# Mixing expert weights on TensorE in column quarters, with the first load in four parts

## The chip, the cores and the metric

The kernel runs on one core of a Trainium2 chip. A core has four engines that compute (TensorE, short PE, multiplies matrices; VectorE, DVE; ScalarE, ACT; GpSimd, POOL) and a fifth, SyncE (SP), that here only issues DMA transfers. Each engine works through its own instructions in order and waits on semaphores for the others. The metric is the device time of one execution in microseconds, the median over several runs.

## The reference

Four layers are applied to x, of 4 images with 512 channels of 64 x 64 points, all in float32. Only layer 1 has to be seen in detail:

```python
# layer 0: attention inside each image, 64 channels wide: softmax over 4096 x 4096 scores
x = scale * (w_out @ (value @ softmax(key.T @ query))) + x
# layer 1: a convolution block whose weights are mixed per image from E = 8 experts
rw = sigmoid(mean(x) @ router_w.T + router_b)         # [image, expert]
W  = einsum('be,eoihw->boihw', rw, experts)           # for each of w1, w2, w3
x  = relu(bn(conv1x1(relu(bn(conv3x3(relu(bn(conv1x1(x, W1))), W2))), W3)) + x)
# layer 2: linear attention;  layer 3: projection, two discounted running sums, a gate
```

w1 has 128 x 512 weights per expert, w2 128 x 128 x 9 and w3 512 x 128. The mixing of experts is a sum over e of rw[b, e] times the weights of expert e; it can only start when the mean over the image of layer 0's output is known.

## The kernel before

The function `unshifted` does the work. `tile_kernel` calls it, and then a second, slower form only if a range test fails, which it doesn't here. TensorE's instructions stand in the order in which the program text issues them (`manual_schedule` around the loop over images, line 859). VectorE's stand in program order inside the blocks marked so; elsewhere, and for ScalarE in layers 0 to 2, a scheduler orders them.

An image is held as four x tiles of 128 x (4 x 1024), one per pair of 512-point blocks ("pr" 0 to 3). Images after the first are loaded during layer 3 of the image before. For the first, `load_pair` (line 81) issues one 2 MB transfer per tile, after the 384 KB of wqkv_sb; the projection in `project_in` (line 170) takes 128 channels (kc) of a tile at a time.

Experts are stored as 17 pieces ("j") of 128 input rows x 8 experts x 128 output columns: 4 for w1, 9 for w2, 4 for w3. Their mixing takes two forms:

- Pieces 0 to 3 are loaded early in layer 0 (ex0, line 159). At the end of layer 0, lines 329 to 337 make rw from the pooled sums, lines 338 to 340 make eight diagonal matrices rw[e] * identity on VectorE, and TensorE sums diag[e] times the expert's pieces over e in PSUM (line 345). ScalarE copies the result to wc (line 360).
- Pieces 4 to 16 go through `mix_experts` (line 361): a load, one scaled copy on ScalarE (line 365), and seven multiply-adds on VectorE (line 367). It runs for pieces 4 to 6, 7 to 9 and 10 to 12 in layer 1, and for 13 to 16 (w3) as `mix_last`, placed after `sums_of_six(2)` (line 566).

conv1 (line 395) multiplies the x tiles with pieces 0 to 3, all four pairs one after another; ScalarE writes h1. conv2 is a 3 x 3 convolution by a fast algorithm along the rows: `sums_of_six` (line 408, VectorE) makes six combinations of h1, lines 382 to 388 make combinations of the nine pieces of w2 (taps), TensorE multiplies (line 448), VectorE combines back (lines 451 to 458), ScalarE makes h (line 462). conv3 multiplies with pieces 13 to 16 (line 471), and VectorE adds x (line 473).

Buffers matter to the loads. `bigp` has three buffers, which in layer 0 hold the keys, queries with values, and part of a ring of exponentials; `xpool` has five, four x tiles and another part of the ring. A load of experts waits until one of these is free. In PSUM, `pair_psum` has three buffers of two banks and `bank` two of one bank. At the start of a run, VectorE and ScalarE also make the batch-norm constants (lines 127 to 134), and ScalarE sums the last two x tiles (line 284).

An f32 product appears in the trace as two TensorE instructions, each with its weight load. Where the output takes 64 of the 128 columns, two products on the two halves stand side by side.

Of the kernel before, what the change touches and what calls it, by code (L numbers as in the profile page):

```python
# [8 lines left out]
F32 = mybir.dt.float32  # L9
AF = mybir.ActivationFunctionType  # L10
ALU = mybir.AluOpType
AX = mybir.AxisListType
# [3 lines left out]
P = 128  # L16
HW = H * W
NB = 512
NBLK = HW // NB
ROWS = NB // W  # L20
KC = C // P
# [3 lines left out]
NPAIR = NBLK // 2  # L25
E = 8
NPIECE = KC + 9 + KC
# [16 lines left out]

@with_exitstack
def unshifted(ctx: ExitStack, tc: tile.TileContext, fits, x, wqkv_t, wout_t, router_t,
                experts, wqk_t, wv_t, bv, wproj_t, prm, out):


    nc = tc.nc  # L50
# [24 lines left out]
    def late_weights(src, shape, name):  # L75

        t = wlate.tile(shape, F32, tag="late", name=name)
        nc.sync.dma_start(t, src)
        return t

    def load_pair(b, pr):

        t = xpool.tile([P, KC, 2 * NB], F32, tag="x", name=f"x_{b}_{pr}")
        nc.sync.dma_start(t, x[b, :, pr * 2 * NB:(pr + 1) * 2 * NB].rearrange("(kc p) n -> p kc n", p=P))
        return t


# [54 lines left out]
    def router_of_values():  # L142
# [9 lines left out]
                             start=kc == 0, stop=kc == KC - 1)  # L152
        nc.vector.tensor_scalar(wr_sb, wo_t[:, 1, 0:E], col(SCALE), 1.0 / HW, ALU.mult, ALU.mult)

    def layer0(b, xs):


        tc.keep_in_program_order(nc.scalar.preload_act_table_set("natural_log_exp_and_others"))
        ex0 = late_weights(experts[0:KC].rearrange("n p e c -> p n e c"), [P, KC, E, P], f"ex_{b}_0")
# [158 lines left out]


        pr = NPAIR - 1  # L320
        for i in groups[-1]:
            values(i)
        with tc.manual_schedule(engines={mybir.EngineType.DVE}):
            sums(pr, early=False)
            for m in range(KC):
                y = out_product(pr - 1, m)
                nc.scalar.activation(ring[8 + m], y, AF.Copy, scale=col(SCALE))
            ys = [out_product(pr, m) for m in range(2)]
            prod = small.tile([P, E], F32, tag="prod", name=f"prod_{b}")
            nc.vector.scalar_tensor_tensor(prod, wr_sb, osum[:, 1:2], base, ALU.mult, ALU.add)  # L330
            logit = bank(f"logit_{b}", (P, E))
            nc.tensor.matmul(logit, ones, prod, start=True, stop=True)
            rw = small.tile([P, E], F32, tag="rw", name=f"rw_{b}")
            nc.vector.tensor_tensor(rw, logit, col(RB, E), ALU.add)
            nc.scalar.activation(rw, rw, AF.Exp, scale=-1.0)
            nc.vector.tensor_scalar(rw, rw, 1.0, None, ALU.add)
            nc.vector.reciprocal(rw, rw)
            diag = four(f"diag_{b}").rearrange("p h (e c) -> p (h e) c", c=P)
            for e in range(E):
                nc.vector.tensor_scalar(diag[:, e, :], ident, rw[:, e:e + 1], None, ALU.mult)  # L340
            ys.append(out_product(pr, 2))
            add_out(pr, 0, ys[0])
            mix = bank(f"mix_{b}", (P, KC, P))
            for e in range(E):
                nc.tensor.matmul(mix, diag[:, e, :], ex0[:, :, e, :], start=e == 0, stop=e == E - 1)
# [7 lines left out]
        return rw, mix  # L353

    def layer1(b, xs, rw, mix):

        wcq = bigp.tile([P, NPIECE + 1 + 4 * NPAIR, P], F32, tag="big", name=f"wc_{b}")
        wc = wcq[:, 0:NPIECE, :]
        qs = wcq[:, NPIECE + 1:, :].rearrange("p (a j) c -> p a (j c)", a=NPAIR)
        nc.scalar.copy(wc[:, 0:KC, :], mix)  # L360
        def mix_experts(j, n, pool, tag):
            ex = pool.tile([P, 4, E, P], F32, tag=tag, name=f"ex_{b}_{j}")
            nc.sync.dma_start(ex[:, 0:n], experts[j:j + n].rearrange("n p e c -> p n e c"))
            acc = wc[:, j:j + n, :]
            nc.scalar.activation(acc, ex[:, 0:n, 0, :], AF.Copy, scale=rw[:, 0:1])
            for e in range(1, E):
                nc.vector.scalar_tensor_tensor(acc, ex[:, 0:n, e, :], rw[:, e:e + 1], acc,  # L367
                                               ALU.mult, ALU.add)
# [12 lines left out]
        part = block(f"part_{b}", (P, 4, P))[:, 0:3, :]  # L381
        nc.scalar.activation(taps[:, 0], g0, AF.Copy, scale=0.25)
        for k, c0, c1 in ((1, -1 / 6, 1 / 6), (3, 1 / 24, -1 / 12)):
            c2 = -1 / 6 if k == 1 else 1 / 6
            nc.scalar.activation(part, g0, AF.Copy, scale=c0)
            nc.vector.scalar_tensor_tensor(part, g2, c2, part, ALU.mult, ALU.add)
            nc.vector.scalar_tensor_tensor(taps[:, k], g1, -c1, part, ALU.mult, ALU.add)
            nc.vector.scalar_tensor_tensor(taps[:, k + 1], g1, c1, part, ALU.mult, ALU.add)


        h1 = bigp.tile([P, 4, H, W // 4 + 1], F32, tag="big", name=f"h1_{b}")
# [81 lines left out]
                nc.vector.scalar_tensor_tensor(xm, flat(y), bn_s[:, 2 + m:3 + m], xm, ALU.mult, ALU.add)  # L473
                nc.scalar.activation(xm, xm, AF.Relu, bias=bn_t[:, 2 + m:3 + m])

        return conv1, sums_of_six, lambda: mix_experts(13, 4, bigp, "big"), conv2, conv3, wcq, qs

    def layer2(b, xs, conv1, sums_of_six, mix_last, conv2, conv3, wcq, qs):

        ks = small.tile([P, NPAIR], F32, tag="ks", name=f"ks_{b}")  # L480
        g = bank(f"g_{b}", (P, C))
# [75 lines left out]
        def ahead(pr):  # L557
            return [lambda j=j: move(pr, j) for j in range(2)]

        for pr in range(NPAIR):  # L560
            conv1(pr)
        with tc.manual_schedule(engines={mybir.EngineType.DVE}):
            sums_of_six(0)
            sums_of_six(1)
            sums_of_six(2)
            mix_last()
            h2 = {0: conv2(0)}
            sums_of_six(3)
            h2[1] = conv2(1)
            conv3(0, h2[0])  # L570
# [305 lines left out]

@with_exitstack
def general(ctx: ExitStack, tc: tile.TileContext, x, wqkv_t, wout_t, router_t,
                experts, wqk_t, wv_t, bv, wproj_t, prm, out):

    nc = tc.nc
    const = ctx.enter_context(tc.tile_pool(name="g_const", bufs=1))
# [432 lines left out]
```

## Time and profile before

| | |
|---|---|
| median of 3 runs | 2747.29 us (2745.97 to 2748.14) |
| profiled execution | 2749.85 us |
| its span, first to last instruction | 2748.1 us |
| mean granted TensorE clock | 0.997 |
| instructions in the trace | 25459 |
| mixing on VectorE, line 367, per image | 21 of 128 x 384 at 0.62 us, 7 of 128 x 512 at 0.76 us |
| mixing on TensorE, line 345, per image | 16 instructions, from 310.82 to 317.88 us in the first image |
| first TensorE instruction | 9.16 us |

A row of the page's costliest groups shows how it is written:

```profile
L471 PE MATMUL c<-h,wc 128*128 128x512 f32 x256 | 118.7, 605 | 11.2 <-DVE x L473 5.8
```

Line 471 on TensorE writes the tile c from h and wc, with weights of 128 rows x 128 columns and 512 data columns, 256 times: 118.7 us busy, 605 ns of one; before these, the engine sat idle for 11.2 us, of which VectorE's writing of x at line 473 ended 5.8. The 605 ns overlap with the next instruction, since matmuls are pipelined; the distance between starts is the true pace.

### The profile page before, as it was taken

What the parts mean: (1) busy time and instruction counts of PE and PEld (TensorE: products, weight loads), DVE (VectorE), ACT (ScalarE), POOL (GpSimd) and SP (SyncE); (2) the same over time, 40 slices, a digit from 0 to 9 for tenths busy, and PEclk for the clock granted to TensorE, in tenths of its full rate; (3) what the DMA queues carried; (4) which work ended last, traced back from release to release, by engine and by line L of the source; (5) the groups of instructions that cost most, each with busy time, mean ns of one, the idle gap of its engine ahead of it and who ended that gap; (6) DMA issues with size and microseconds to landing.
All of it is one profiled execution on the core that took longest, in us unless ns stands there. A gap on an engine that the chain in (4) does not pass through costs nothing.

```text
span 2748.1 us, 25459 instructions
## 1 busy us (share of the span) xinstructions
PE 2682.6 (98%) x9918; PEld 1119.6 (41%) x9918; DVE 1991.3 (72%) x2259; ACT 1310.9 (48%) x1491; POOL 10.7 (0%) x26
## 2 busy tenths in 40 slices
PE   8999999999999999999999999999999999999998
PEld 3333354344333345434433334544443333554443
DVE  2688776787478777678747778767874787866787
ACT  4545344445554434345555452534555545252545
POOL 1000000000000000000000000000000000000000
PEclk9999999999999999999999999999999999999999
DMA  4000200022200020002120002101221000200011
GB/s 186 1 1 1 100 31 0 16 88 88 85 1 1 1 100 31 1 16 107 77 77 1 1 1 100 31 1 43 79 96 57 1 1 1 100 31 0 31 44 50
DMA packets 38081, 115.14 MB, mean 42 GB/s; under 512 B 2880, under 2 KB 12096, under 8 KB 37952
## 3 DMA queue, kind: packets, MB, share of 16 engines
q1 hardware_dynamic: 37952, 113.43, 10.9%
q8 instruction: 80, 1.31, 0.2%
q14 instruction: 49, 0.40, 0.0%
HBM read 79.86 MB, written 33.55 MB: 41 GB/s over the span
## 4 chain that ended last, share of the span: by engine, by line
PE 78%; DVE 16%; ACT 3%; issue 1%; DMA 1%; SPq 1%; DVEq 0%; ACTq 0%
PE s L212 17%; PE av L227 16%; PE sx L720 14%; PE zy L720 11%; PE kq L173 4%; PE z L492 2%; DVE wc L367 2%; PE wv L638 2%; PE vv L173 2%; PE g L554 2%; PE xtr L537 2%; PE c L448 1%; PE y L266 1%; PE c L471 1%; DVE x L473 1%
## 5 line engine op out<-in xcount | busy, mean ns | idle before, releaser
L212 PE MATMUL s<-qv,key 64*128 64x512 f32 x2048 | 469.1, 602 | 1.8 <-ACT ring L215 1.8
L220 DVE TENSOR_TENSOR acc<-acc,ring 128x1024 f32<-128x1024 f32 x312 | 381.7, 1223 | 101.1 <-ACT ring L215 72.5
L215 ACT ACTIVATE ring<-s 128x1024 f32<-128x1024 f32 x336 | 317.7, 1038 | 224.1 <-PE s L212 224.0
L227 PE MATMUL av<-ring,qv 128*64 128x512 f32 x1344 | 304.5, 595 | 0.0
L212 PEld LDWEIGHTS s<-qv,key 64*128 64x128 f32 x2048 | 189.2, 187 | 275.0 <-issue 173.7
L220 DVE TENSOR_TENSOR acc<-acc,ringx 128x1024 f32<-128x1024 f32 x168 | 205.5, 1223 | 101.7 <-ACT ringx L215 89.4
L215 ACT ACTIVATE ringx<-s 128x1024 f32<-128x1024 f32 x176 | 172.1, 1040 | 207.0 <-PE s L212 207.0
L720 PE MATMUL sx<-t,sx 128*128 128x512 f32 x512 | 236.8, 596 | 0.0
L227 PEld LDWEIGHTS av<-ring,qv 128*64 128x64 f32 x1344 | 93.3, 137 | 198.6 <-issue 198.6
L227 PE MATMUL av<-ringx,qv 128*64 128x512 f32 x704 | 167.2, 597 | 0.0
L725 ACT COPY zy<-sx 128x512 f32<-128x512 f32 x64 | 36.5, 570 | 240.1 <-PE sx L720 230.6
L770 DVE TENSOR_TENSOR_SCAN t<-sx,t 128x512 f32<-128x512 f32 x128 | 148.9, 1210 | 1.7
L720 PEld LDWEIGHTS sx<-t,sx 128*128 128x128 f32 x512 | 95.7, 190 | 128.0 <-issue 121.3
L759 ACT COPY t<-s 128x1024 f32<-128x1024 f32 x64 | 127.1, 1992 | 40.5 <-DVE s L753 40.5
L753 DVE TENSOR_TENSOR_SCAN s<-wc,s 128x512 f32<-128x512 f32 x128 | 146.0, 1204 | 0.0
L729 ACT ACTIVATE e<-sx,prm_sb 128x512 f32<-128x512 f32 x128 | 86.9, 686 | 123.9 <-PE sx L720 123.8
L471 PE MATMUL c<-h,wc 128*128 128x512 f32 x256 | 118.7, 605 | 11.2 <-DVE x L473 5.8
L776 ACT ACTIVATE s<-t 128x1024 f32<-128x1024 f32 x64 | 125.4, 1985 | 1.0 <-DVE t L770 0.9
L173 PE MATMUL kq<-x,wqkv_sb 128*64 128x512 f32 x512 | 116.1, 607 | 9.3 <-DMA x<-in_x_dram 9.2
L720 PE MATMUL sx<-t,wq 128*128 128x512 f32 x256 | 117.0, 597 | 7.5 <-ACT e L729 7.5
L720 PE MATMUL zy<-t,wq 128*128 128x512 f32 x256 | 118.7, 604 | 2.5 <-ACT zy L725 2.5
L720 PE MATMUL zy<-x,wq 128*128 128x512 f32 x256 | 116.2, 594 | 0.0
(191 smaller groups left out, 3443.1 us busy)
## 6 DMA issues: line engine op xcount, KB each, us to landing
x<-in_x_dram SPq DMA_DIRECT2D x16, 2048.0 KB, 8.4
out_dram<-s SPq DMA_DIRECT2D x64, 512.0 KB, 2.6
ex<-in_experts_dram SPq DMA_DIRECT2D x12, 1536.0 KB, 10.5
ex<-in_experts_dram SPq DMA_DIRECT2D x8, 2048.0 KB, 7.7
wq<-in_wproj_t_dram SPq DMA_DIRECT2D x32, 256.0 KB, 4.7
wv_sb<-in_wv_t_dram SPq DMA_DIRECT2D x1, 1024.0 KB, 9.6
wqkv_sb<-in_wqkv_t_dram SPq DMA_DIRECT2D x1, 384.0 KB, 3.4
wout_sb<-in_wout_t_dram SPq DMA_DIRECT2D x2, 128.0 KB, 13.9
```

Source lines behind the costliest of these rows:

```text
L173: nc.tensor.matmul(y[h * D:(h + 1) * D, :], wqkv_sb[:, kc, col0:col0 + D], xs[pr][:, kc, h * NB:(h + 1) * NB], start=kc == 0, stop=kc == K ...
L212: nc.tensor.matmul(s[:, h, :], key[r, kt * P:(kt + 1) * P], qry[r, pr * NB:(pr + 1) * NB], start=True, stop=True)
L215: nc.scalar.activation(p, s, AF.Exp)
L220: nc.vector.tensor_tensor(accs[pr], accs[pr], p, ALU.add)
L227: nc.tensor.matmul(avs[pr][h * D:(h + 1) * D, :], vt[:, kt, :], ring[i % RING][:, h, :], start=kt == 0, stop=kt == NT - 1)
L471: nc.tensor.matmul(y[:, h, :], wc[:, KC + 9 + m, :], h2[:, h, :], start=True, stop=True)
L720: nc.tensor.matmul(y, w[:, c, self.kind, self.j * P:(self.j + 1) * P], v[:, c, :], start=c == 0 and k in (1, 5), stop=c == 1, skip_group_c ...
L729: nc.scalar.activation(self.e[k], self.x, AF.Identity, bias=self.bias[k - 2])
L753: nc.vector.tensor_tensor_scan(self.half(i, h), along[:, self.j + 2 * i, :], self.half(i, h), 0.0, ALU.mult, ALU.add)
L759: nc.scalar.copy(self.t[i].rearrange("p (w r) -> p w r", w=W), self.s[i].rearrange("p (r w) -> p w r", w=W))
L770: nc.vector.tensor_tensor_scan(th, down[:, i, :], th, 0.0, ALU.mult, ALU.add)
L776: nc.scalar.activation(self.s[i].rearrange("p (r w) -> p w r", w=W), tw, AF.Sigmoid)
```

## The change

The diff makes two changes.

All 17 pieces are mixed on TensorE. The experts are stored a second time on the host as `packed`: partition 32 * e' + i of a piece holds row i of four experts at once (e' = 0 to 3, in two groups g), for each of the four 32-row blocks q of the piece. A selector `sel` of 128 x 32 per group has rw of expert 4g + e' at the places (32 e' + i, i). One product of `sel` with block q sums four experts for 32 rows; its output goes to partitions 32q to 32q + 31, a quarter of the array's columns; two groups accumulate. `mix` issues eight such products per load and a ScalarE copy from PSUM. `mix_experts` and `mix_last`, the diagonals, and their work on ScalarE and VectorE go. Loads become `load_experts`, issued earlier in the program: pieces 4 to 6 before the last values of layer 0, 7 to 9 and 10 to 12 after them, 13 to 16 after conv1's second block. conv1 moves from layer 2's function into layer 1's, with the last two mixes between its blocks.

The first tile of the first image is loaded in four transfers of 512 KB, one per 128 channels.

```diff
+        src = x[b, :, pr * 2 * NB:(pr + 1) * 2 * NB].rearrange("(kc p) n -> p kc n", p=P)
+        if b == 0 and pr == 0:
+            for kc in range(KC):
+                nc.sync.dma_start(t[:, kc, :], src[:, kc, :])
+        else:
+            nc.sync.dma_start(t, src)
...
+    which = const.tile([P, 4], F32, tag="which", name="which")
+    nc.vector.tensor_reduce(which, ident.rearrange("p (e i) -> p e i", e=4), AX.X, ALU.add)
+    row = const.tile([P, 32], F32, tag="row", name="row")
+    nc.vector.tensor_reduce(row, ident.rearrange("p (e i) -> p i e", e=4), AX.X, ALU.add)
...
+    def load_experts(b, j, n, pool, tag):
+        ex = pool.tile([P, n, 4, 2, P], F32, tag=tag, name=f"ex_{b}_{j}")
+        nc.sync.dma_start(ex, packed[:, j:j + n])
+        return b, j, n, ex
+
+    def mix(wc, sel, experts):
+        b, j, n, ex = experts
+        y = bank(f"mix_{b}_{j}", (P, n, P))
+        for g in range(2):
+            for q in range(4):
+                nc.tensor.matmul(y[32 * q:32 * (q + 1)], sel[:, g, :], ex[:, :, q, g, :], start=g == 0, stop=g == 1,
+                                 tile_position=(0, 32 * q))
+        nc.scalar.copy(wc[:, j:j + n, :], y)
...
+        ex4 = load_experts(b, 4, 3, bigp, "big")
         for i in groups[-1]:
             values(i)
+        ex7 = load_experts(b, 7, 3, xpool, "x")
+        wcq = bigp.tile([P, NPIECE + 1 + 4 * NPAIR, P], F32, tag="big", name=f"wc_{b}")
+        ex10 = load_experts(b, 10, 3, bigp, "big")
...
-            diag = four(f"diag_{b}").rearrange("p h (e c) -> p (h e) c", c=P)
-            for e in range(E):
-                nc.vector.tensor_scalar(diag[:, e, :], ident, rw[:, e:e + 1], None, ALU.mult)
+            own = small.tile([P, 2, 4], F32, tag="own", name=f"own_{b}", bufs=1)
+            nc.vector.tensor_tensor(own, rw.rearrange("p (g e) -> p g e", g=2),
+                                    which[:, None, :].to_broadcast([P, 2, 4]), ALU.mult)
+            part = small.tile([P, 2], F32, tag="part", name=f"part_{b}", bufs=1)
+            nc.vector.tensor_reduce(part, own, AX.X, ALU.add)
+            sel = small.tile([P, 2, 32], F32, tag="sel", name=f"sel_{b}", bufs=1)
+            for g in range(2):
+                nc.vector.tensor_scalar(sel[:, g, :], row, part[:, g:g + 1], None, ALU.mult)
             ys.append(out_product(pr, 2))
             add_out(pr, 0, ys[0])
-            mix = bank(f"mix_{b}", (P, KC, P))
-            for e in range(E):
-                nc.tensor.matmul(mix, diag[:, e, :], ex0[:, :, e, :], start=e == 0, stop=e == E - 1)
+            mix(wcq, sel, ex0)
             ys.append(out_product(pr, 3))
...
-        nc.scalar.copy(wc[:, 0:KC, :], mix)
-        def mix_experts(j, n, pool, tag):
-            ex = pool.tile([P, 4, E, P], F32, tag=tag, name=f"ex_{b}_{j}")
-            nc.sync.dma_start(ex[:, 0:n], experts[j:j + n].rearrange("n p e c -> p n e c"))
-            acc = wc[:, j:j + n, :]
-            nc.scalar.activation(acc, ex[:, 0:n, 0, :], AF.Copy, scale=rw[:, 0:1])
-            for e in range(1, E):
-                nc.vector.scalar_tensor_tensor(acc, ex[:, 0:n, e, :], rw[:, e:e + 1], acc,
-                                               ALU.mult, ALU.add)
-
-        mix_experts(4, 3, bigp, "big")
-        mix_experts(7, 3, xpool, "x")
-        mix_experts(10, 3, bigp, "big")
+        mix(wc, sel, ex4)
+        mix(wc, sel, ex7)
...
+        conv1(0)
+        mix(wc, sel, ex10)
+        sums_of_taps()
+        conv1(1)
+        ex13 = load_experts(b, 13, KC, bigp, "big")
+        conv1(2)
+        mix(wc, sel, ex13)
+        conv1(3)
...
-        for pr in range(NPAIR):
-            conv1(pr)
         with tc.manual_schedule(engines={mybir.EngineType.DVE}):
             sums_of_six(0)
             sums_of_six(1)
             sums_of_six(2)
-            mix_last()
...
+        "packed": experts.reshape(NPIECE, 4, 32, 2, 4, P).transpose(4, 2, 0, 1, 3, 5).reshape(P, NPIECE, 4, 2, P),
```

`sums_of_taps` holds the former lines 381 to 388 unchanged.

More of the change, by code (lines that the diff above doesn't have):

```diff
@@ L46, in unshifted @@
 def unshifted(ctx: ExitStack, tc: tile.TileContext, fits, x, wqkv_t, wout_t, router_t,
-                experts, wqk_t, wv_t, bv, wproj_t, prm, out):
+                experts, packed, wqk_t, wv_t, bv, wproj_t, prm, out):
     nc = tc.nc
@@ L83, in load_pair @@
         t = xpool.tile([P, KC, 2 * NB], F32, tag="x", name=f"x_{b}_{pr}")
-        nc.sync.dma_start(t, x[b, :, pr * 2 * NB:(pr + 1) * 2 * NB].rearrange("(kc p) n -> p kc n", p=P))
+        src = x[b, :, pr * 2 * NB:(pr + 1) * 2 * NB].rearrange("(kc p) n -> p kc n", p=P)
[4 more added lines that the diff above has]
+            nc.sync.dma_start(t, src)
         return t
@@ L153, in router_of_values @@
         nc.vector.tensor_scalar(wr_sb, wo_t[:, 1, 0:E], col(SCALE), 1.0 / HW, ALU.mult, ALU.mult)
+    def load_experts(b, j, n, pool, tag):
[10 more added lines that the diff above has]
+        nc.scalar.copy(wc[:, j:j + n, :], y)
     def layer0(b, xs):
         tc.keep_in_program_order(nc.scalar.preload_act_table_set("natural_log_exp_and_others"))
-        ex0 = late_weights(experts[0:KC].rearrange("n p e c -> p n e c"), [P, KC, E, P], f"ex_{b}_0")
+        ex0 = load_experts(b, 0, KC, wlate, "late")
         key = bigp.tile([P, HW], F32, tag="big", name=f"key_{b}")
@@ L352, in layer0, with layer1 @@
             sum_range(pr)
-        return rw, mix
-    def layer1(b, xs, rw, mix):
-        wcq = bigp.tile([P, NPIECE + 1 + 4 * NPAIR, P], F32, tag="big", name=f"wc_{b}")
+        return wcq, sel, ex4, ex7, ex10
+    def layer1(b, xs, wcq, sel, ex4, ex7, ex10):
         wc = wcq[:, 0:NPIECE, :]
         qs = wcq[:, NPIECE + 1:, :].rearrange("p (a j) c -> p a (j c)", a=NPAIR)
-        nc.scalar.copy(wc[:, 0:KC, :], mix)
-        def mix_experts(j, n, pool, tag):
-            ex = pool.tile([P, 4, E, P], F32, tag=tag, name=f"ex_{b}_{j}")
-            nc.sync.dma_start(ex[:, 0:n], experts[j:j + n].rearrange("n p e c -> p n e c"))
-            acc = wc[:, j:j + n, :]
-            nc.scalar.activation(acc, ex[:, 0:n, 0, :], AF.Copy, scale=rw[:, 0:1])
-            for e in range(1, E):
-                nc.vector.scalar_tensor_tensor(acc, ex[:, 0:n, e, :], rw[:, e:e + 1], acc,
-                                               ALU.mult, ALU.add)
-        mix_experts(4, 3, bigp, "big")
-        mix_experts(7, 3, xpool, "x")
-        mix_experts(10, 3, bigp, "big")
+        mix(wc, sel, ex4)
+        mix(wc, sel, ex7)
         wl = wlate.tile([P, 2 * HW // 2], F32, tag="late", name=f"wl_{b}")
@@ L380, in layer1, with sums_of_taps @@
         u5 = g2
[L381 to L388, printed above, removed]
+        def sums_of_taps():
+            part = block(f"part_{b}", (P, 4, P))[:, 0:3, :]
+            nc.scalar.activation(taps[:, 0], g0, AF.Copy, scale=0.25)
+            for k, c0, c1 in ((1, -1 / 6, 1 / 6), (3, 1 / 24, -1 / 12)):
+                c2 = -1 / 6 if k == 1 else 1 / 6
+                nc.scalar.activation(part, g0, AF.Copy, scale=c0)
+                nc.vector.scalar_tensor_tensor(part, g2, c2, part, ALU.mult, ALU.add)
+                nc.vector.scalar_tensor_tensor(taps[:, k], g1, -c1, part, ALU.mult, ALU.add)
+                nc.vector.scalar_tensor_tensor(taps[:, k + 1], g1, c1, part, ALU.mult, ALU.add)
         h1 = bigp.tile([P, 4, H, W // 4 + 1], F32, tag="big", name=f"h1_{b}")
@@ L474, in conv3, with layer2 @@
                 nc.scalar.activation(xm, xm, AF.Relu, bias=bn_t[:, 2 + m:3 + m])
-        return conv1, sums_of_six, lambda: mix_experts(13, 4, bigp, "big"), conv2, conv3, wcq, qs
-    def layer2(b, xs, conv1, sums_of_six, mix_last, conv2, conv3, wcq, qs):
+        conv1(0)
[6 more added lines that the diff above has]
+        conv1(3)
+        return sums_of_six, conv2, conv3, wcq, qs
+    def layer2(b, xs, sums_of_six, conv2, conv3, wcq, qs):
         ks = small.tile([P, NPAIR], F32, tag="ks", name=f"ks_{b}")
@@ L878, in general @@
 def general(ctx: ExitStack, tc: tile.TileContext, x, wqkv_t, wout_t, router_t,
-                experts, wqk_t, wv_t, bv, wproj_t, prm, out):
+                experts, packed, wqk_t, wv_t, bv, wproj_t, prm, out):
     nc = tc.nc
@@ L1286 @@
     w3 = l1["w3"].reshape(E, KC, P, P).transpose(1, 3, 0, 2)
+    experts = np.concatenate([w1, w2, w3], axis=0)
     prm = np.concatenate(
@@ L1297 @@
         "router_t": l1["router_w"].T,
-        "experts": np.concatenate([w1, w2, w3], axis=0),
+        "experts": experts,
+        "packed": experts.reshape(NPIECE, 4, 32, 2, 4, P).transpose(4, 2, 0, 1, 3, 5).reshape(P, NPIECE, 4, 2, P),
         "wqk_t": np.concatenate([a["L2_conv_Wq"], a["L2_conv_Wk"]], axis=0).T,
```

## The prediction

> **What bounds the kernel now.** I read the page first, then TensorE's rows in order of time around the change, then VectorE's rows and the start. The page, its engine and chain-of-waits lines:
>
> ```profile
> PE 2682.6 (98%) x9918; PEld 1119.6 (41%) x9918; DVE 1991.3 (72%) x2259; ACT 1310.9 (48%) x1491; POOL 10.7 (0%) x26
> ...
> PE 78%; DVE 16%; ACT 3%; issue 1%; DMA 1%; SPq 1%; DVEq 0%; ACTq 0%
> ```
>
> TensorE (PE) is busy 98% and still only 78% of the chain; VectorE (DVE) has 16%. So TensorE sets the end, with stretches where it waits for VectorE or is just caught by it. Only its idle time can be won, and every microsecond added to its own work is paid. Its rows in order of time, first image (start, length, engine, line, count, idle before):
>
> ```profile
> 310.82 7.13 PE L345 MATMUL mix<-ex,diag 128*128 128x512 f32 x16 [0.21 <-DVE diag L340]
> 317.88 1.13 PE L266 MATMUL y<-o,wout_sb 64*128 64x512 f32 x4
> 318.94 27.73 PE L399 MATMUL c<-x,wc 128*128 128x512 f32 x64
> 346.51 5.24 PE L448 MATMUL c<-v,wl 128*128 128x256 f32 x24
> ...
> 362.73 4.04 PE L471 MATMUL c<-h,wc 128*128 128x512 f32 x8 [0.68 <-ACT h L462]
> 367.34 1.96 PE L471 MATMUL c<-h,wc 128*128 128x512 f32 x4 [0.57 <-DVE sp L452]
> 370.71 1.98 PE L471 MATMUL c<-h,wc 128*128 128x512 f32 x4 [1.41 <-DVE x L473]
> 372.53 5.34 PE L448 MATMUL c<-v,wl 128*128 128x256 f32 x24
> ```
>
> Take pace from starts, since ends are modelled: 64 instructions from 318.94 to 346.51 are 0.43 us each. An f32 product is two such instructions (conv1 has 32 products), so 128 weight columns over 512 data columns cost 0.86 us. By that pace conv2 (two blocks of 36 half-width instructions, 0.215 each) ends at 361.99, and the next starts at 362.73: 0.74 us lost. Eight instructions end at 366.17, next at 367.34: 1.17. Four end at 369.06, next at 370.71: 1.65. Together **3.56 us** lost, by waits that lead to VectorE. The same three gaps stand at 1042, 1722 and 2400 us in the other images. VectorE's rows for the same time:
>
> ```profile
> 327.01 8.74 DVE L367 SCALAR_TENSOR_TENSOR wc<-ex,rw,wc 128x384 f32<-128x384 f32 x14
> ...
> 352.29 5.47 DVE L367 SCALAR_TENSOR_TENSOR wc<-ex,rw,wc 128x512 f32<-128x512 f32 x7
> 357.68 0.68 DVE L451 TENSOR_TENSOR dq<-c,sp 128x512 f32<-128x512 f32 x1
> ```
>
> The reader sees why: VectorE mixes experts for 5.47 us just when conv2's first block waits to be combined (line 451), so h, and with it conv3, is late.
>
> **The change, part by part.**
>
> *Removed from VectorE.* 28 multiply-adds per image: 21 at 0.62 us and 7 at 0.76, 18.3 us, and eight diagonals, 1.66 us. ScalarE loses four scaled copies (0.61, two in 1.12, 0.72) and gains five PSUM copies near the old 0.58; it idles 12.47 us at 332. Most of these 20 us are no gain, as VectorE waits for TensorE later anyway (4.30 us idle at 378.53). What counts is the 3.56 us.
>
> *What is late next.* I replay the order. conv1 ends at 346.51 + 1.55 (the three additions below), 348.1. conv2's first block then gives its first PSUM bank at 353.3; the ScalarE copy (0.59) and VectorE's seven combining steps (3.7 us) end at 357.5, after c2e at 355.9; h at 360.0 (two ScalarE steps, 2.48). The fourth sums of six take 4.5 us, to 362.0. conv3 starts at 363.6, so h waits 3.6 us for it. conv3's PSUM buffer returns after one 1.28 us VectorE step, against 1.72 us that TensorE spends on one; the second combination ends at 365.7, the first conv3 result at 365.3. All three gaps go: **-3.56**.
>
> *TensorE work.* Removed: 16 x 0.43 = 6.88. Added, per image: five mixes of eight products, each two instructions. Columns are 512 for the mixes of four pieces (two of them) and 384 for the three of three pieces: 32 x 0.43 + 48 x 0.3225 = 29.24 us if one runs at a time. The trace has no quarter-width product. The nearest rows are the half-width ones, in the chain of waits:
>
> ```profile
> 277.22 5.30 PE av L227 x24
> 282.52 5.35 PE s L212 x24
> ```
>
> 24 instructions of 512 columns in 5.30 us are 0.22 each, half of 0.43: two halves run side by side in full. Bounds: two at a time 29.24 / 2 = 14.62; four at a time 29.24 / 4 = 7.31. I take 7.31, since the halves show no loss from sharing: **+0.43**. Here a rule speaks against it. The Trainium skill, TensorE: Matmul & The Clock Gate, Part 3, gives measured speedups of 3.07 for four row tiles and 2.38 for three column tiles. By 3.07 the mixes cost 9.52, +2.64 and not +0.43, 8.8 us more over four images. The row of the halves reaches 2.0 of 2, so I follow the row and keep the rule as a case; no row here shows four.
>
> *Mode switches.* 12 slots of 0.43 are 5.16, so the two rows above carry 0.14 and 0.19 for a change of the array's division. Before, this stretch had three such points (y to mix, mix to y, y to conv1), 0.2 each, 0.6. After: y to mix, mix to y, y to mix (two mixes in a row), mix to conv1, then in and out twice more: eight, some 1.32. **+0.72**. Bounds 0 and 1.
>
> *The selector.* Before, the first mix starts 0.06 us after the first diagonal (310.48 + 0.28). Now four small dependent VectorE steps stand there (product, reduction, two scalings); such steps follow each other by 0.22 (336 to 337 to 340 start at 310.03, 310.24, 310.48). Ready near 311.3: **+0.4**. All PE work queues behind this wait, so it is paid whole.
>
> *Loads.* Same bytes, contiguous. Three loads were issued at 302.15 and all landed before 316 (4.7 MB at about 0.42 MB/us). The first of them now waits only for the keys' buffer (last scores 295.0) and needs 3.8 us; its mix comes at 314. The next two are in by 312, needed at 315.5 and 324. The last, 2 MB, 5 us, can start when the fourth mix frees a buffer (325.4) and is needed near 339.3; if this cover went it would stop TensorE. Nothing else is in SP's queue from 303 to 395, so no transfer is held up. GpSimd's zeroing of h1, which waited for line 367 until about 332, is ready by 316; conv1's first output is at 324. A mix's PSUM bank is copied by ScalarE in 0.6 us while conv1 runs; only the third mix follows closely and it uses the other bank.
>
> *Moving conv1* between mixes shifts VectorE's needed inputs: conv1's third block reads x with the line 351 sums, ready at 320.7, needed at 332. Free.
>
> Sum: -3.56 + 0.43 + 0.72 + 0.4 = -2.01 per image, **-8.0 for four**.
>
> *First load in parts.* The start, rows of three engines:
>
> ```profile
> 9.16 9.98 PE L173 MATMUL kq<-x,wqkv_sb 128*64 128x512 f32 x32 [9.16 <-DMA x<-in_x_dram]
> ...
> 24.43 0.29 DVE L128 TENSOR_SCALAR bn_v<-prm_sb 128x1 f32<-128x1 f32 x3 [1.13 <-DMA prm_sb<-in_prm_dram]
> ...
> 28.73 0.21 ACT L129 ACTIVATE bn_s<-bn_v 128x6 f32<-128x6 f32 x1
> ...
> 32.91 0.68 DVE L194 COPY qv<-kq 128x512 f32<-128x512 f32 x1
> ...
> 33.64 7.09 PE L173 MATMUL kq<-x,wqkv_sb 128*64 128x512 f32 x32 [0.18 <-DVE qv L194]
> ```
>
> The 2 MB land at 9.1; at 0.42 MB/us the last three quarters take 3.75, so the first is there at 5.4. A quarter feeds two slots of 0.855 (the pace of the first six us), 1.7 us, and the next comes after 1.25, so TensorE does not starve: it starts 3.75 us earlier. Three more issues on SP at 0.5 us delay the later x loads' issue, not their data: the queue is full until 23 us. But the third pair is held at 33.64 by a VectorE copy, in line behind bn steps that wait for prm (24.43, does not move) and for ScalarE's square root. ScalarE's five accumulations before it start at 18.6, when their x lands, instead of 21.55, so root and copy move 2.6 us: I take **-2.6**; bounds -1 and -4.5. The skill's same page, Part 1, says the slow clock lasts until a free-running 3.4 us window was busy. The trace shows the half pace from 9.16 to about 15, 5.9 us. By the row nothing changes; by the rule the stretch may be 3.4 to 6.8, 5.1 on average, -0.4. I keep the row. The profile also grants half clock from 66.2 to 73, after TensorE idled 3.2 us; by that rule it may not recur (-3.4), which I leave to the range.
>
> Two small reductions for the selector's masks lie in VectorE's idle start: free. Total -8.0 - 2.6 = -10.6. The profiled execution took 2749.85 (span 2748.1 and 1.75 around it), giving 2739.25; its excess of 2.56 over the median 2747.29 is run to run, so the median goes to **2736.7**.
>
> **The rivals.**
> 1. *More goes as well*: no half clock at 66 us, or layer 2's own gaps (at 409, 419, 428, together 2.7 us per image) shrink because the scheduler orders VectorE anew. For it: line 659 there blocks VectorE 8.56 us for a load. Against: that order is local and untouched. 2725 to 2733, middle 2730. Chance 0.12.
> 2. *Quarters share worse*, factor 3.07: 2736.7 + 8.8 = 2745.5, no change that can be told. 0.07.
> 3. *A new wait takes the old one's place* at conv3: work +1.55 per image and no gain, 6.2 - 2.6: 2750.9. Against: 3.6 us of slack for h in the replay. 0.04.
> 4. *Slower: quarters run two at a time or singly*, so TensorE pays for the mixing that VectorE did beside it. Place: the five mixes. Two at a time cost 14.62 instead of 7.31, 29.2 over four images: 2765.9 (0.09); one at a time 21.9 per image more, 2824 (0.03; then the change does not do what it says). It decides below 29.24 / (7.31 + 10.6 / 4) = 2.9 at a time. For it: only two were ever shown.
>
> **How the numbers follow.** The forecast has 0.65. A measurement tells 0.2% (5.5 us) from no change. Faster by more: forecast and 1, 0.77; within: 2 and 3, 0.11; slower: 4, 0.12. The forecast's own bounds are 2731 to 2742; the range goes down into case 1 and up over case 2: 2726 to 2748, which leaves out cases 3 and 4 and the far tails.
>
> **What would show it.** Each mix of 512 columns should start-to-next-start in about 1.9 us with 16 instructions in four groups of four; pairs would show 3.6. conv3's rows at 362 us should have no idle before them. PE's first row should start near 5.4 and the third pair near 31. VectorE's total should fall by about 75 us and ScalarE's little. A row of TensorE waiting for a mix's selector, its load or its PSUM bank for over 1 us per image would prove me wrong, as would conv3 still waiting for h.

## The result and the profile after

The changed kernel takes 2735.83 us (median of 4 runs, 2734.66 to 2737.18); the kernel before, measured beside it, 2747.72 (2745.97 to 2748.53). The ratio is **0.9958, interval 0.9941 to 0.9975**: faster by 0.4%. The profiled execution took 2737.18 us with a span of 2735.4, 12.67 less than before.

The page of the changed kernel, its engine line and its chain of waits:

```profile
PE 2682.8 (98%) x10174; PEld 1116.4 (41%) x10174; DVE 1918.6 (70%) x2133; ACT 1310.5 (48%) x1491; POOL 10.7 (0%) x26
...
PE 87%; DVE 8%; ACT 2%; issue 1%; DMA 1%; SPq 1%; DVEq 0%; ACTq 0%
```

VectorE lost 72.7 us of work and TensorE gained 0.2 in sum, yet the kernel won only 12.67: nearly all of VectorE's work had stood beside TensorE's. VectorE's share of the chain fell from 16 to 8%, some 220 us, which is no measure of the gain either. The gain is found in TensorE's rows, first image (start, length, engine, line, count, idle before):

```profile
307.22 1.92 PE L176 MATMUL mix<-ex,sel 128*32 128x512 f32 x16 [0.56 <-DVE sel L374]
309.07 1.13 PE L291 MATMUL y<-o,wout_sb 64*128 64x512 f32 x4
310.13 2.79 PE L176 MATMUL mix<-ex,sel 128*32 128x384 f32 x32
312.85 7.13 PE L421 MATMUL c<-x,wc 128*128 128x512 f32 x16
319.92 1.50 PE L176 MATMUL mix<-ex,sel 128*32 128x384 f32 x16
321.34 14.00 PE L421 MATMUL c<-x,wc 128*128 128x512 f32 x32
335.27 1.92 PE L176 MATMUL mix<-ex,sel 128*32 128x512 f32 x16
337.13 7.13 PE L421 MATMUL c<-x,wc 128*128 128x512 f32 x16
344.10 5.24 PE L470 MATMUL c<-v,wl 128*128 128x256 f32 x24
...
358.18 1.46 PE L470 MATMUL c2e<-wl,wc 128*128 128x256 f32 x6
359.48 7.03 PE L493 MATMUL c<-h,wc 128*128 128x512 f32 x16
366.35 5.34 PE L470 MATMUL c<-v,wl 128*128 128x256 f32 x24
```

The reader sees two things. A mix of 16 instructions of 512 columns lasts 1.85 us from its start to the next start (307.22 to 309.07): four groups of four. And conv3's first row at 359.48 has no idle before it, and its 16 instructions run in one stretch; before, they came in pieces. I call the time from the first `logit` product to layer 2's first product z "layer 1's stretch". It was 85.70, 85.70, 85.69 and 85.60 us in the four images and is 83.47 in each. The first image came to its `logit` 3.95 us earlier (309.17 to 305.22). The two together are -12.76; the rest changed by about 0.1.

VectorE at the same place, the changed kernel:

```profile
341.53 0.42 DVE L440 SCALAR_TENSOR_TENSOR wl<-t,t 128x256 f32<-128x256 f32 x1
349.99 0.69 DVE L473 TENSOR_TENSOR dq<-c,sp 128x512 f32<-128x512 f32 x1 [8.04 <-ACT sp L472]
```

VectorE now idles 8.04 us before it may combine conv2's first block. That is far more than needed to remove a wait of TensorE, and TensorE paid for it. This is what the experiments follow up.

The start, TensorE of the changed kernel:

```profile
5.43 1.98 PE L198 MATMUL kq<-x,wqkv_sb 128*64 128x512 f32 x4 [5.43 <-DMA x<-in_x_dram]
8.02 8.95 PE L198 MATMUL kq<-x,wqkv_sb 128*64 128x512 f32 x28 [0.61 <-DMA x<-in_x_dram]
20.23 7.03 PE L198 MATMUL kq<-x,wqkv_sb 128*64 128x512 f32 x32
...
31.22 7.09 PE L198 MATMUL kq<-x,wqkv_sb 128*64 128x512 f32 x32
```

In this execution TensorE begins 3.7 us earlier but stops between 7.17 (by the pace of starts) and 8.02, as the second part is not there. The third pair starts at 31.22 instead of 33.64.

### The profile page after: what moved, and what is told of

It is laid out like the page before. It is cut to its first block, busy times and chain, and to the rows that moved or that the text cites. A ratio compares the mean times of both kernels' runs of the same rounds, so it can differ in the third digit from the quotient of the medians.

```text
span 2735.4 us, 25841 instructions
## 1 busy us (share of the span) xinstructions
PE 2682.8 (98%) x10174; PEld 1116.4 (41%) x10174; DVE 1918.6 (70%) x2133; ACT 1310.5 (48%) x1491; POOL 10.7 (0%) x26
## 4 chain that ended last, share of the span: by engine, by line
PE 87%; DVE 8%; ACT 2%; issue 1%; DMA 1%; SPq 1%; DVEq 0%; ACTq 0%
PE s L237 17%; PE av L252 16%; PE sx L747 14%; PE zy L747 11%; PE kq L198 4%; PE c L421 4%; PE c L470 3%; PE c L493 2%; PE z L522 2%; PE vv L198 2%; PE wv L665 2%; PE g L584 2%; PE xtr L567 2%; PE y L291 2%; PE c2e L470 2%; PE mix L176 1%
## 5 line engine op out<-in xcount | busy, mean ns | idle before, releaser
L747 PE MATMUL sx<-x,wq 128*128 128x512 f32 x256 | 116.2, 594 | 0.0
```

The lines of the kernel that those rows point to most:

```text
L747: nc.tensor.matmul(y, w[:, c, self.kind, self.j * P:(self.j + 1) * P], v[:, c, :], start=c == 0 and k in (1, 5), stop=c == 1, skip_group_c ...
```

## The experiments

All of these kernels compute the whole reference. Times are medians; each ratio is against the kernel before, run beside it on the same chip.

| what is run | us | before | ratio and interval | layer 1's stretch, first image |
|---|---|---|---|---|
| the change | 2735.83 | 2747.72 | 0.9958 [0.9941, 0.9975] | 83.47 |
| first load in parts alone | 2744.75 | 2748.17 | 0.9991 [0.9984, 0.9997] | 85.67 |
| mixing alone | 2740.58 | 2748.17 | 0.9970 [0.9959, 0.9980] | 83.46 |
| quarter by quarter | 2736.21 | 2748.17 | 0.9959 [0.9944, 0.9974] | 83.70 |
| pieces 13 to 16 on VectorE | 2729.67 | 2748.17 | 0.9934 [0.9919, 0.9949] | 81.41 |
| pieces 4 to 12 on VectorE | 2753.50 | 2747.24 | 1.0023 [1.0012, 1.0034] | 87.6 |
| 7 to 9 and 13 to 16 on VectorE | 2721.78 | 2747.24 | 0.9909 [0.9892, 0.9925] | 79.79 |
| the same, router's steps apart | 2712.34 | 2747.24 | 0.9872 [0.9856, 0.9889] | 79.79 |
| the same, two load parts | 2712.68 | 2747.24 | 0.9875 [0.9858, 0.9891] | 79.79 |
| router apart, 4 to 12 on VectorE, loads in time | 2709.30 | 2748.23 | 0.9868 [0.9850, 0.9887] | 79.13 |
| router apart, 4 to 9 and 13 to 16 on VectorE | 2711.09 | 2748.23 | 0.9869 [0.9852, 0.9885] | 79.29 |
| 4 to 16 on VectorE, change of 0 to 3 kept | 2737.35 | 2747.99 | 0.9962 [0.9948, 0.9976] | 83.42 |

### The two parts alone

Into the kernel before, only this:

```diff
+        if b == 0 and pr == 0:
+            for kc in range(KC):
+                nc.sync.dma_start(t[:, kc, :], src[:, kc, :])
+        else:
+            nc.sync.dma_start(t, src)
```

> The kernel before with only the first x tile loaded in four parts. Theory (as read from the trace of after): TensorE starts 3.7 us earlier, loses 0.9 us waiting for the second part and 0.7 us to a longer half clock, so the third pair starts 2.2 to 2.6 us earlier; the half-clock stretch near 66 us may be 3.4 or 6.8 us long by chance, worth up to 1.7 us. Time 2.2 to 4.2 us below before, 2743.5 to 2745.5; layers 1 to 3 unchanged to 0.1 us per image. Rival (the prediction's own reason): the batch-norm constants on VectorE hold the third pair, gain limited by them; then VectorE's rows for bn stand before the third pair's copy and TensorE waits there.

By the medians it brought 3.4 us. The profiled execution, however, took 2749.34, the second slowest of 21, so its trace shows what can go wrong and not the usual run. TensorE, and then the VectorE copy that the fourth pair waits for:

```profile
8.80 8.79 PE L178 MATMUL kq<-x,wqkv_sb 128*64 128x512 f32 x28 [1.08 <-DMA x<-in_x_dram]
...
45.27 7.09 PE L178 MATMUL kq<-x,wqkv_sb 128*64 128x512 f32 x32 [2.32 <-DVE qv L199]
```

```profile
44.53 0.69 DVE L199 COPY qv<-kq 128x512 f32<-128x512 f32 x1 [6.23 <-ACT key L198]
```

The second part came at 8.80 and stopped TensorE for about a microsecond. The third pair started at 31.84 without a wait for VectorE. The fourth (45.27) did wait 2.32 us for a VectorE copy, but VectorE itself had been idle for 6.23 us: it waited for ScalarE's copy of the keys, which began at 42.14, in line behind the square root for the bn constants (37.10) and three accumulations. The first image's `logit` came only 0.88 us earlier than before (308.29).

The reverse, the change with the first tile in one transfer:

```diff
-        if b == 0 and pr == 0:
-            for kc in range(KC):
-                nc.sync.dma_start(t[:, kc, :], src[:, kc, :])
-        else:
-            nc.sync.dma_start(t, src)
+        nc.sync.dma_start(t, src)
```

> The change without the split first load. Theory: the first TensorE instruction is back at 9.1 us, the third pair at about 33.6, and each image keeps the 2.2 us between the logit and layer 2's first product (83.5 us against 85.7): 8.9 us below before, 2738.8. Rival: if the two parts of the change help each other (other order on VectorE at the start), the gain differs from 8.9 by over 1 us.

The median fell by 7.6 us and the profiled span by 9.6 (2748.1 to 2738.5), with single runs from 2737.29 to 2741.57. The median alone is 1.3 us short of the theory's 8.9, more than the 1 us that the rival names, but its interval (5.5 to 11.3 us) can't tell the two apart. Layer 1's stretch was 83.46, as in the full change, so the 2.2 us per image belong to the mixing alone. The two parts together give 11.0 of the 11.9 us by which the medians of the change differ; within these spreads they add up.

### Does the order of the quarters matter?

```diff
-        for g in range(2):
-            for q in range(4):
+        for q in range(4):
+            for g in range(2):
```

> The change with the two loops of the mix exchanged: all products of one quarter, then of the next, the same 40 products per image. Theory: TensorE starts instructions in program order, so four quarters only run side by side when neighbours in the order are on different quarters; here a mix of 512 columns takes up to 6.9 us instead of 1.85, 21.9 us more per image if nothing overlaps, 16 us more if the last pass of one quarter overlaps the first of the next: 2800 to 2824. Rival: each quarter has a queue of its own and the order does not matter: 2735.8.

The theory was wrong; the time is the rival's. TensorE of this kernel, the first mix:

```profile
306.77 2.09 PE L176 MATMUL mix<-ex,sel 128*32 128x512 f32 x16 [0.55 <-DVE sel L374]
308.79 1.13 PE L291 MATMUL y<-o,wout_sb 64*128 64x512 f32 x4
```

A mix lasts 2.02 us instead of 1.85, though products to the same quarter follow each other in the program. Singly it would be 16 x 0.43 = 6.88. Its first four instructions start between 306.77 and 306.95, the next four between 307.23 and 307.41. All five mixes together cost 0.23 us more per image. The quarters work side by side in either order; why the order matters so little (the rival's own queue per quarter, for instance) no run here shows.

### Which of VectorE's work made conv3 late?

The prediction named the 5.47 us of pieces 13 to 16 beside conv2. Put back alone, with 0 to 12 left on TensorE:

```diff
-        ex13 = load_experts(b, 13, KC, bigp, "big")
         conv1(2)
-        mix(wc, sel, ex13)
         conv1(3)
...
             sums_of_six(2)
+            mix_last()
             h2 = {0: conv2(0)}
```

> The change, but pieces 13 to 16 are mixed on VectorE at the old place (5.5 us between the third sums of six and conv2's combining), pieces 0 to 12 on TensorE. Theory: the three gaps of conv3, 3.6 to 3.8 us per image, come from these 5.5 us alone and return; TensorE saves 2.0 us for the missing mix, so each image is 1.7 us longer than in the change: 2742.5. Rival: the gaps came from VectorE's load as a whole (18.3 us), and with 13 us still gone they stay away: 2.0 us shorter per image, 2728.

It was faster than the change. VectorE, and then TensorE, of this kernel:

```profile
340.91 5.47 DVE L395 SCALAR_TENSOR_TENSOR wc<-ex,rw,wc 128x512 f32<-128x512 f32 x7
346.97 0.69 DVE L485 TENSOR_TENSOR dq<-c,sp 128x512 f32<-128x512 f32 x1 [0.59 <-ACT sp L484]
```

```profile
355.16 1.46 PE L482 MATMUL c2e<-wl,wc 128*128 128x256 f32 x6
356.45 7.03 PE L505 MATMUL c<-h,wc 128*128 128x512 f32 x16
363.32 5.34 PE L482 MATMUL c<-v,wl 128*128 128x256 f32 x24
```

The same seven multiply-adds stand at the same place of the program, but end at 346.38, and VectorE still waits 0.59 us before it combines. conv3 has no gap. TensorE saves one mix of about 1.85 us per image, and layer 1's stretch falls by 2.06. So the 5.47 us alone were not the cause.

Then the other way round, with pieces 4 to 12 on VectorE and 13 to 16 on TensorE:

```diff
-        mix(wc, sel, ex4)
-        mix(wc, sel, ex7)
+        mix_experts(4, 3, ex4)
+        mix_experts(7, 3, ex7)
+        mix_experts(10, 3, ex10)
...
         conv1(0)
-        mix(wc, sel, ex10)
```

> The change, but pieces 4 to 12 are mixed on VectorE (21 multiply-adds, 13.1 us) and pieces 0 to 3 and 13 to 16 on TensorE. Theory (backlog): what counts is when VectorE has finished the sums of six, not what stands beside conv2. VectorE ends its last sum over x near logit + 12.5, the mixing at + 25.7, taps and first sums at + 33, second sums at + 37.4; conv2 would be ready at + 34.5 and waits about 3 us. Logit to layer 2's first product 82.0 us per image against 83.5 in the change, time near 2730. Rival (place): only the 5.5 us beside conv2 ever cost anything, so no wait here: 79.0 us per image, 2718.

This run was slower than before, but tested neither theory. Its queue of transfers on SP, and TensorE:

```profile
329.67 0.34 SPq L167 DMA_DIRECT2D ex<-in_packed_dram  x1
```

```profile
337.11 3.64 PE L181 MATMUL mix<-ex,sel 128*32 128x512 f32 x16 [6.05 <-DMA ex<-in_packed_dram]
340.68 7.81 PE L434 MATMUL c<-x,wc 128*128 128x512 f32 x16
```

The load of pieces 13 to 16 could only be issued at 329.67, since VectorE's mixing held its buffer until 329.6. TensorE waited 6.05 us for the data (about 6 in each image) and was granted half clock (0.50 in the profile) from 335.27 to 342.09, 6.83 us: the mix took 3.57 us (337.11 to 340.68), not 1.85. The question was taken up again below, with the buffer freed earlier.

### A split that fits VectorE's free time

After the change VectorE is idle for 8 us before conv2. Two sets go back to it, 7 to 9 and 13 to 16; TensorE mixes 0 to 6 and 10 to 12 in one run ahead of conv1:

```diff
         mix(wc, sel, ex4)
-        mix(wc, sel, ex7)
+        mix(wc, sel, ex10)
+        mix_experts(7, 3, ex7)
...
         conv1(0)
-        mix(wc, sel, ex10)
         sums_of_taps()
         conv1(1)
-        ex13 = load_experts(b, 13, KC, bigp, "big")
         conv1(2)
-        mix(wc, sel, ex13)
         conv1(3)
...
             sums_of_six(2)
+            mix_last()
```

> Pieces 7 to 9 and 13 to 16 on VectorE, 0 to 6 and 10 to 12 on TensorE in one run of mixes ahead of conv1. Theory: VectorE has 4.2 us idle before the first sums of six, which takes 4.4 us of mixing, and room for the last set as in the run with that set on VectorE; TensorE saves one mix and two changes of division, 1.5 us per image more than there: logit to layer 2's first product 79.9 us (81.4 there), time near 2723.5. Rival: the idle stretch is not usable (the load of 7 to 9 lands late, or the first sums are pushed back to conv2): 81 us or more, 2728 or more.

Layer 1's stretch is 79.79 us, 3.68 below the change, as the theory said (79.9).

On top of this kernel, the router's small products, at which TensorE waited 3.2 us near 64 us, were put apart between score products:

```diff
                 scores(i)
+                if i == 0:
+                    v_transpose(*pend)
+                elif i == 1 and b == 0:
+                    router = router_of_values()
+                elif i == 3 and b == 0:
+                    router_products(*router)
             if g == 0:
-                v_transpose(*pend)
-                if b == 0:
-                    router_of_values()
```

> As the run with two sets on VectorE, and in the first image the router's transposes go after the second score product and its small products after the fourth, with the last value transpose after the first. Theory: TensorE's wait of 3.2 us near 60 us and the half clock of 3.4 to 6.8 us that follows it go, 4.9 to 6.6 us: 2717 to 2719. Rival: the scores in this group are bound by ScalarE's exponentials or by PSUM buffers anyway, and part comes back as waits there: gain below 3 us.

It brought 9.4 us, more than the theory's 4.9 to 6.6. TensorE, first in the change, then in this kernel:

```profile
64.06 1.28 PE L161 MATMUL wo_t<-router_sb,wot_sb 128*128 128x8 f32 x8 [3.19 <-DVE wot_sb L159]
```

```profile
56.37 1.99 PE L245 MATMUL s<-qv,key 64*128 64x512 f32 x8
58.29 1.06 PE L164 MATMUL wo_t<-router_sb,wot_sb 128*128 128x8 f32 x8
59.27 7.14 PE L245 MATMUL s<-qv,key 64*128 64x512 f32 x32
```

The wait of 3.19 us is gone. With it goes the half clock: none is granted from 12.71 us until TensorE has ended (2699.66). The rest came from the moved value transpose, the only one of the moved steps that acts in every image. From the first score product to `logit`, images two to four took 245.85 us each in the kernel with two sets on VectorE and take 244.56 here, 1.29 less; the first image took 251.98 and takes 246.45, 5.53 less. Together that is 9.4, the gain of the medians.

With two load parts of 1 MB instead of four:

```diff
-            for kc in range(KC):
-                nc.sync.dma_start(t[:, kc, :], src[:, kc, :])
+            for kc in range(0, KC, 2):
+                nc.sync.dma_start(t[:, kc:kc + 2, :], src[:, kc:kc + 2, :])
```

> As the run with the router apart, with the first tile loaded in two transfers of 1 MB in place of four of 512 KB. Theory: four parts in one queue share the 16 DMA engines, so the second lands at 8.0 to 8.8 us, when most of the whole is in, and TensorE starves for 0.9 to 1.4 us and stays at half clock longer; with two parts it starts near 6.8 us and does not starve, and the second pair starts within 0.5 us of the four-part run: same time to 1 us. Rival: the parts are strictly in order and four are better by 1.2 us.

TensorE began at 6.73 and no longer stopped; the second pair started at 18.82 instead of 20.02, the first `logit` at 298.36 instead of 299.54. The medians can't be told apart. Nor do four parts always stop TensorE: in the next two kernels, which load in four, the second pair started at 18.11 and 18.21.

### The middle on VectorE again, with its loads in time

On top of the kernel with the router apart, 4 to 12 on VectorE in the order 4, 10, 7, which frees a `bigp` buffer early; 13 to 16 on TensorE behind conv1:

```diff
-        mix(wc, sel, ex4)
-        mix(wc, sel, ex10)
+        mix_experts(4, 3, ex4)
+        mix_experts(10, 3, ex10)
         mix_experts(7, 3, ex7)
...
+        ex13 = load_experts(b, 13, KC, bigp, "big")
         conv1(2)
         conv1(3)
+        mix(wc, sel, ex13)
...
             sums_of_six(2)
-            mix_last()
```

> The version with the router apart, but with pieces 4 to 12 mixed on VectorE (13.1 us) and 0 to 3 and 13 to 16 on TensorE; the load of 13 to 16 gets a buffer that VectorE frees early, and its mix stands after conv1's fourth block, so that the load is in time (the run with the middle on VectorE lost 6 us per image to that load and a half clock after it). Theory (backlog): VectorE is late at conv2's combining only when both the 13.1 us and the 5.5 us are on it; with the 13.1 us alone the third sums of six end 40.5 us after the logit and the combining can start 40.6 us after it, so no gap at conv3. Logit to layer 2's first product 79.0 us per image against 79.8: 2709. Rival: the 13.1 us by themselves make conv2 or conv3 wait: 80.5 us or more, 2715 or more.

This is the lowest median, 2709.30 us (single runs 2708.06 to 2718.03), and as the theory said (79.0 us per image, 2709). TensorE of this kernel:

```profile
302.54 27.73 PE L440 MATMUL c<-x,wc 128*128 128x512 f32 x64
330.21 1.92 PE L184 MATMUL mix<-ex,sel 128*32 128x512 f32 x16
332.06 5.34 PE L489 MATMUL c<-v,wl 128*128 128x256 f32 x24
...
347.54 7.03 PE L512 MATMUL c<-h,wc 128*128 128x512 f32 x16
```

conv1 is again one run of 27.7 us, the mix follows without a wait for its load, and conv3 has no gap. So the 13.1 us of pieces 4 to 12 alone do not make VectorE late enough to stop TensorE either.

One set fewer on TensorE, with 0 to 3 and 10 to 12 there and all else on VectorE:

```diff
-        mix(wc, sel, ex4)
         mix(wc, sel, ex10)
+        mix_experts(4, 3, ex4)
         mix_experts(7, 3, ex7)
```

> The version with the router apart, with pieces 4 to 9 and 13 to 16 on VectorE (14.2 us) and only 0 to 3 and 10 to 12 on TensorE. Theory: TensorE saves one mix of 384 columns, 1.3 us; VectorE ends its last set about 2 us after conv2's first result, inside the 3.6 us by which h is early, so at most 0.5 us comes back: 79.0 us per image, 2709. Rival: the 2 us late combining moves through the second combining to conv3's PSUM buffers and costs 1 to 2 us: 79.5 to 80.5 us, 2711 to 2715.

The first small gap returns. TensorE, and then VectorE:

```profile
331.65 5.24 PE L489 MATMUL c<-v,wl 128*128 128x256 f32 x24
...
352.86 1.98 PE L512 MATMUL c<-h,wc 128*128 128x512 f32 x4 [0.52 <-DVE x L514]
```

```profile
339.84 0.68 DVE L492 TENSOR_TENSOR dq<-c,sp 128x512 f32<-128x512 f32 x1
```

From conv2's start to z it takes 0.8 us longer than the change (1.1 in the third image), between the theory's 0.5 and the rival's 1 to 2.

### All of 4 to 16 on VectorE

From the change, only pieces 0 to 3 keep their quarters:

```diff
-        mix(wc, sel, ex4)
-        mix(wc, sel, ex7)
+        mix_experts(4, 3, ex4)
+        mix_experts(10, 3, ex10)
+        mix_experts(7, 3, ex7)
...
             sums_of_six(2)
+            mix_last()
```

> The change with only pieces 0 to 3 mixed on TensorE in quarters and all others, 4 to 16, on VectorE as in the kernel before (18.6 us). TensorE's own work is 5 us per image less than before. Theory (backlog): VectorE decides, its combining for conv2 starts at the same point as before but for 0.8 us (the diagonals that are gone), so TensorE's 5 us turn into waits ahead of conv2 and conv3: logit to layer 2's first product 84.5 to 85.5 us against 85.7 before, 83.5 in the change; time near 2741 with the split load's 3.4 us, or up to 3 us per image more where the wait brings a half clock. Rival: TensorE's work sets this stretch and VectorE's lateness costs only the 3.6 us seen before: 80.7 us per image, 2725.

The result lies between the two figures. VectorE and TensorE of this kernel:

```profile
347.75 5.47 DVE L400 SCALAR_TENSOR_TENSOR wc<-ex,rw,wc 128x512 f32<-128x512 f32 x7
353.14 0.68 DVE L486 TENSOR_TENSOR dq<-c,sp 128x512 f32<-128x512 f32 x1
```

```profile
358.19 6.86 PE L506 MATMUL c<-h,wc 128*128 128x512 f32 x12 [3.25 <-ACT h L497]
366.17 1.98 PE L506 MATMUL c<-h,wc 128*128 128x512 f32 x4 [1.12 <-DVE x L508]
```

TensorE reaches conv2 4.9 us sooner than before (32.48 us after `logit`, not 37.34), because the first four pieces cost it a quarter. VectorE does not finish as much sooner, so conv3 waits 3.25 and 1.12 us, and a stretch of 3.41 us at half clock comes with the wait in each image (6.83 in the last). Of the 4.9 us, 2.3 remain: just what the whole change brought per image.

## Why the prediction was right, and where it was not

**The number.** Forecast 2736.7, measured 2735.83; the range held it, and the likeliest case occurred. That the two lie within 1 us is partly luck: layer 1 gave 8.8 us instead of 8.0, and the start differs by some 4 us between traces of kernels that begin alike (below).

**The terms of layer 1**, first image:

| term | predicted | measured | from |
|---|---|---|---|
| gaps at conv3 | -3.56 | -3.77 | conv2's start to z: 48.36 (346.51 to 394.87), now 44.59 (344.10 to 388.69) |
| mixes and mode switches | +1.15 | +1.19 | mixes 7.06, now 1.85 + 2.72 + 1.42 + 1.86 = 7.85; conv1 27.57, now 7.07 + 13.93 + 6.97 = 27.97 |
| the selector's wait | +0.4 | +0.35 | last y to mix: 0.47, now 0.82 |
| sum | -2.01 | -2.23 | |

*How wide the quarters run.* The prediction had to choose between the row of halves, which shared without loss, and the rule of the Trainium skill, TensorE: Matmul & The Clock Gate, Part 3, Measured speedup vs the span model, with 3.07 for four row tiles. By the rule a 512-column mix would take an estimated 6.88 / 3.07 = 2.24 us; it takes 1.85 with its change of mode, and 2.02 even in the worse order. The measurement decides: four column quarters of this kernel run four at a time.

*Loads, PSUM banks, ScalarE.* No mix of the changed kernel waited for its load or its bank, and ScalarE's total moved by 0.4 us.

**The step that failed.** The prediction said that VectorE mixes experts for 5.47 us "just when conv2's first block waits", so that these are why conv3 is late. The replay that took all gaps away was sound, for all mixing left VectorE; the attribution was not. Taking that row's pieces alone off VectorE does leave conv3 whole (4 to 12 on VectorE, loads in time), but so does keeping it and taking the others off (13 to 16 on VectorE). A row next to a wait is not its whole cause if the engine reached that row late. The test is when VectorE gets free against when conv2's first block can be combined. In the change this is 349.99 - 344.10 = 5.89 us after conv2's first product. The table has VectorE's lateness by that measure, and by how much the stretch from conv2's first product to z is longer than the change's 44.59 us:

| mixed on VectorE | VectorE late by | stretch longer by |
|---|---|---|
| nothing (the change) | -8.0 | 0.0 |
| 13 to 16 | -0.6 | 0.0 |
| 7 to 9 and 13 to 16 | -0.6 | 0.0 |
| 4 to 12, loads in time | +0.5 | 0.1 |
| 4 to 9 and 13 to 16 | +2.3 | 0.8 |
| 4 to 16 (before) | +5.3 | 3.8 |
| 4 to 16, TensorE 4.9 us sooner | +7.9 | 6.3 |

In the last three rows the two columns differ by 1.5 us each time (5.28 - 3.76, 2.30 - 0.78, 7.86 - 6.34; all their images but one lie between 1.4 and 1.5, that one at 1.2). So VectorE may be about 1.5 us late without loss, and all beyond is paid in full; the half clock in the last row adds nothing to that. By that estimate, removing about 3.8 us of VectorE's 18.3 before conv2 (5.3 - 1.5) would have closed the gaps, as long as TensorE came no sooner. No run tried just this. The change took all 18.3, and TensorE pays about 1.4 us for each set of three pieces and 1.85 for the last. That is why 72.7 us off VectorE became 8.8 us in layer 1, and why the better splits gain about 4 us more per image.

**The start.** The size was nearly right in the profiled execution (third pair -2.6 predicted, -2.42 measured), but not by the reasons given, and partly by luck.

- The next part "comes after 1.25" us, "so TensorE does not starve". In this execution it did, for 0.86 us. The trace has sixteen landings for each part, as many as the core has DMA engines, and TensorE started only after the last of them. Those of the first part came between 4.73 and 5.29 us, those of the second between 6.20 and 7.98, half of them by 6.7. The queue's rate thus gave the middle of the sixteen (5.4 + 1.25), not the last. How late the last one is differs from trace to trace; ten of the kernels profiled load in four parts:

| last landing of the second part | traces | TensorE's stop | half pace until | third pair starts |
|---|---|---|---|---|
| 7.27 to 7.81 | six | 0 to 0.3 | 9.4 to 11.0 | 29.1 to 29.9 |
| 7.98 to 8.76 | four, the change among them | 0.7 to 1.3 | 12.7 to 14.0 | 31.0 to 31.8 |

- That the third pair "is held at 33.64 by a VectorE copy, in line behind bn steps" was to be the brake. In the changed kernel that copy is ahead of the bn steps, and the third pair does not wait for it:

```profile
29.70 0.69 DVE L219 COPY qv<-kq 128x512 f32<-128x512 f32 x1 [8.56 <-ACT key L218]
31.36 0.28 DVE L138 TENSOR_SCALAR bn_v<-prm_sb 128x1 f32<-128x1 f32 x3
```

What really took away part of the 3.7 us were the stop and the clock: half pace lasted from 5.43 to 13.54, 8.1 us, against 5.9 before. With luck in the landings the same load brings the third pair 3.8 to 4.6 us forward. The range that the prediction left aside for the half pace, 3.4 to 6.8 us, holds in the nine traces whose start has a stop of at most 0.3 us (3.6 to 5.9 us); with a longer stop it was 6.7 to 8.3. The order of VectorE's steps, which I had taken as given, is set by the scheduler and differs between the kernels.

**The half clock near 66 us** was left to the range. It recurred, for half the time. Stretches of before, then of the change (start:end, length, busy and count of PE, PEld, DVE, ACT, POOL, then the granted clock, DMA share, GB/s):

```profile
66.20:69.00 2.80, 2.53 (x10) 2.29 (x12) 0.44 (x2) 0.00 (x0) 0.00 (x0) 0.50 0.00 0
69.00:73.00 4.00, 4.00 (x12) 1.66 (x10) 1.23 (x1) 1.91 (x2) 0.00 (x0) 0.50 0.00 0
```

```profile
62.50:66.20 3.70, 2.15 (x10) 1.69 (x12) 1.73 (x3) 0.00 (x0) 0.00 (x0) 0.80 0.00 0
66.20:73.00 6.80, 6.80 (x30) 2.69 (x28) 4.24 (x4) 5.31 (x6) 0.00 (x0) 0.86 0.00 0
```

0.50 from 66.2 to 73 before; 0.80 and 0.86, a mean over part of each stretch, after: the half clock lay between 64.74 and 68.16, 3.41 us instead of 6.83. About 1.5 us of the gain at the first `logit` (3.95 - 2.42) is this. It should not be counted as the change's, since the wait of 3.19 us is the same. Five traces that share their code up to there show both effects at that `logit`: with the late second part it stood at 305.22 after the short half clock (the change) and 306.91 after the long one (4 to 16 on VectorE); without it, at 303.13 after the short one (two sets on VectorE), and at 304.25 and 304.77 after the long one (13 to 16 on VectorE; quarter by quarter). The Trainium skill's page named above, Part 1, What's actually happening, has a free-running window of 3.4 us; the lengths seen here, 3.41 and 6.83, are one and two of it.

**Left open.** Whether the better versions differ among themselves: 2709.30, 2711.09, 2712.34 and 2712.68 lie within each other's intervals. Not tried: the best split with two load parts.

## What to carry to other kernels

Before work is moved from a helper to the engine that sets the end, compare when the helper gets free with when its result is needed, over the whole stretch and not at the row beside the wait; move only the excess, since the rest is paid in full. A gap of the main engine is worth its own length, and here those of 3.2 us or more also brought a half clock; so small dependent steps should be put apart between other work. A load in parts helps by when the last share of its second part lands, not only by its first, and a gain of a few microseconds at the start should be read from several executions.

## What the runs showed of the hardware that was not expected

- Four quarter-width products run side by side whether the program names the quarters in turn or one quarter's products in a row: 1.85 and 2.02 us for 16 instructions of 512 columns, against 6.88 singly.
- Transfers issued one after another on one queue don't land evenly. The sixteen shares of the first of four 512 KB parts landed within 0.6 us (4.73 to 5.29), those of the second within 1.8 (6.20 to 7.98); over ten traces the last share of the second part came between 7.27 and 8.76.
- Waits of TensorE of 3.18 to 6.5 us each came with 3.41 or 6.83 us at half clock; one of 2.32 us (first load in parts alone) did not. In the four kernels without such a wait no half clock was granted from the start until TensorE had ended, near 2700 us.
